# First pair of a two-layer graph network: adjacency loaded at once, evictions shared by two engines, weights loaded behind the first gather

## The chip, the cores and the metric

The kernel runs on one core of one Trainium2 chip. A time is the device time of one execution in microseconds (us). Three executions were timed; the profile is of a further one. Engines are called PE (TensorE, matmuls), DVE (VectorE), ACT (ScalarE), POOL (GpSimd) and SP (SyncE, which here only issues transfers). Each engine works through its own instructions strictly in the order in which they were built; a transfer is issued by the queue of SP, ACT or POOL.

## The reference

There are 16 graphs of 1024 nodes with 64 features each, and a symmetric 0/1 adjacency matrix in 32-bit floats (4 MB per graph). Two layers are computed; both begin with `h = max(layernorm(x), 0)` and end with `x = x + layer(h, adj)`.

```
# layer 0: a neighbourhood quantile
neigh = (adj > 0) without the diagonal;  nb = neighbours per node
skip  = ceil(nb/2) where nb > 10: every skip-th neighbour is struck out, symmetrically
s     = the features of the remaining neighbours (and the node itself), sorted per feature
agg   = 0.25*quantile(s, .25) + 0.5*quantile(s, .5) + 0.25*quantile(s, .75)
y     = relu((h + agg) @ W1 + b1) @ W2 + b2
# layer 1: three graph convolutions, each with a batch norm, then a linear map
x1 = bn1(relu(adj @ (h @ W1) + b1));  x2 = bn2(... x1 ...);  x3 = bn3(... x2 ...)
y  = relu(concat(x1, x2, x3) @ Wl + bl)
```

## The kernel before, in words

The 16 graphs are worked on in 8 pairs, `p` from 0 to 7; a graph of a pair is `x` = 0 or 1. The 1024 nodes of a graph are 8 blocks of 128 (`NT` = 8, index `t` or `u`).

`prepare(p, pools)` makes ready what the sort of a pair needs. It loads the features into `room`, computes the layer norm, stores the result in `h_d`, and then for each graph runs `prepare_one`:

1. For each of 8 blocks: load 128 rows of the adjacency (512 KB) into a tile `a`, of which there are two buffers; ACT takes the sign of it into `edge` (one byte each, L662); DVE compares it with 0 and 1 for a flag (`junk_v`, L664); PE transposes it into `ptE` (L669); ACT evicts this from PSUM into `edgeT` (L672).
2. `edgeT` is stored in `adjT_d` (1 MB, L676), and then its diagonal is struck out on DVE (L678, here called the mask of graph x), which has to wait for that store. `chunk_sums` makes partial column sums on PE (`tot`), which ACT evicts (`sums`, L648).
3. For each block: PE computes running counts (`cs`), ACT and DVE turn them into `stays` (L717, L718).
4. For each block: PE sums `q`, ACT evicts it into `edge` with a row sum `nv` (L744).
5. DVE makes sort keys (L750), PE spreads them (`keys`), and ACT compares all nodes with them, block by block (`junk`, L762). From the counts DVE computes `place` (L765), and POOL sends the rows of `edge` to `live_d` in sorted order (L770).

`find_live` (one per graph) loads these rows back (`lp`, L786, two buffers), transposes them on PE (`pt`, L796), evicts them to `liveT` on ACT (L799), and computes the counts `nvs`. `number_slots(side)` numbers the neighbours on PE (`pr`) and evicts them on ACT into `r` (L838): side 0 (`r0`, 592 columns) before the gather, side 1 (`r1`, 432 columns) beside it.

`gather_block` picks features by matmul: DVE builds selections `s` from `r` (L962), PE multiplies them with the features `hp` into `pg` (L993), ACT evicts into `g`. `sort_block` sorts `g` on DVE by a network of minima and maxima between `g` and `t` (L920) and takes the quantiles with coefficients from ACT.

The steps of the next pair's `prepare` are woven between the blocks of the current pair. The first pair has nothing to hide behind: `ahead.rest()` runs its `prepare` to the end, and only then comes `gather_block(st, 0, pools)`. A scheduler orders the instructions of each engine; the `yield`s only mark where a step ends. After the last pair's preparation, `later` runs both layers' dense part; there alone are the weights used.

The weights are loaded ahead of everything, by 53 transfers on ACT's queue in `weight`, `column`, `row` and `both`; the batch norm's factor `s` is computed from them with a square root on ACT (L530). Tiles come from pools: `g`, `t` (pool `rows`), `s`, `agg` (pool `work`) first hold something in the first gather and sort.

Of the kernel before, what the change touches and what calls it, by code (L numbers as in the profile page):

```python
# [21 lines left out]
P = 128  # L22
C = 64
HID = 128
LN_EPS = 1e-5
BN_EPS = 0.001
# [373 lines left out]
def graph_layers_kernel(ctx: ExitStack, tc: tile.TileContext, ins, out: bass.AP):  # L400
# [93 lines left out]
    def weight(name, rows, cols, twice=False):  # L494
        t = const.tile([rows * (1 + twice), cols], F32, name=f"w_{name}")
        for k in range(1 + twice):
            nc.scalar.dma_start(out=t[k * rows : (k + 1) * rows, :], in_=ins[name])
        return t

    def column(name, rows, twice=False):  # L500
        t = const.tile([rows * (1 + twice), 1], F32, name=f"c_{name}")
        for k in range(1 + twice):
            nc.scalar.dma_start(out=t[k * rows : (k + 1) * rows, :], in_=ins[name].rearrange("(p o) -> p o", o=1))
        return t

    def row(name, cols):
        t = const.tile([P, cols], F32, name=f"r_{name}")
        nc.scalar.dma_start(out=t, in_=ins[name].partition_broadcast(P))
        return t

    def both(t, src):

        nc.vector.memset(t, 0.0)
        for k in range(2):
            half = slice(k * C, (k + 1) * C)
            nc.scalar.dma_start(out=t[half, half], in_=src)


    w1 = weight("L0_gnn_W1", C, HID, True)
    w2 = weight("L0_gnn_W2", HID, C)  # L520
    b1 = column("L0_gnn_b1", HID)
    b2 = row("L0_gnn_b2", C)
    layers = []
    for i in (1, 2, 3):
        wl = const.tile([P, P], F32, name=f"wl{i}")
        both(wl, ins[f"L1_gnn_W{i}"])
        bl, g, be, m, v = (column(f"L1_gnn_{k}{i}", C, True) for k in ("b", "g", "be", "m", "v"))
        s = const.tile([P, 1], F32, name=f"bn_s{i}")
        nc.vector.tensor_scalar(s, v, BN_EPS, None, ALU.add)
        nc.scalar.activation(s, s, AF.Sqrt)  # L530
        nc.vector.reciprocal(s, s)
        nc.vector.tensor_tensor(s, s, g, ALU.mult)

        nc.vector.tensor_tensor(m, m, s, ALU.mult)
        nc.vector.tensor_tensor(be, be, m, ALU.subtract)
        layers.append((wl, bl, s, be))
    wlast = const.tile([P, 3, P], F32, name="wlast")
    for i in range(3):
        both(wlast[:, i, :], ins["L1_gnn_Wl"][i * C : (i + 1) * C, :])
    blast = row("L1_gnn_bl", C)  # L540

    biases = {}

# [36 lines left out]
        pass  # L580


    def prepare(p, pools):
# [12 lines left out]
        yield  # L596
        st.g = {}
        st.nvs = keep.tile([P, N], F32, tag="nvs", name="nvs")
# [24 lines left out]
        nc.scalar.copy(st.hp[:, 1], h)  # L623
        nc.vector.tensor_tensor(st.hp[:, 2], h, st.hp[:, 1], ALU.subtract)
        yield
        for x in range(2):
            yield from number_slots[x](1)
        return st

    def diagonal(e):  # L630

        dims = [list(d) for d in e.ap]
        return bass.AP(tensor=e.tensor, offset=e.offset, ap=[dims[0], [N + P, NT], [1, P]])
# [17 lines left out]
    def prepare_one(st, x, pools):  # L651
# [5 lines left out]
        edge = work.tile([P, NT, N], F8, tag="byte", bufs=4, name="edge")  # L657
        edgeT = work.tile([P, NT, N], F8, tag="byte", bufs=4, name="edgeT")
        for t in range(NT):
            a = work.tile([P, N], F32, tag="a", bufs=2, name="a")  # L660
            nc.sync.dma_start(out=a, in_=adj_d[b, t * P : (t + 1) * P, :])
            nc.scalar.activation(edge[:, t, :], a, AF.Sign, saturate=False)  # L662
            junk = work.tile([P, N], F8, tag="junk_v", name="junk_v")
            nc.vector.scalar_tensor_tensor(  # L664
                junk, a, 1.0, a, ALU.is_equal, ALU.not_equal, accum_out=odd[:, b, t : t + 1], saturate=False
            )
            pt = ps.tile([P, NT, P], F32, tag="big", bufs=2, name="ptE")
            for u in range(NT):
                nc.tensor.matmul(  # L669
                    out=pt[:, u, :], lhsT=edge[:, t, u * P : (u + 1) * P], rhs=ident_h, start=True, stop=True  # L670
                )
            nc.scalar.activation(edgeT[:, :, t * P : (t + 1) * P], pt, AF.Copy, saturate=False)  # L672
            if t % 2:
                yield

# [47 lines left out]
        for t in range(NT):  # L723
            q = ps.tile([P, N], F32, tag="big", bufs=2, name="q")
            for hf in range(NH):
                sl = slice(hf * HALF, (hf + 1) * HALF)
                own = slice(t * P, (t + 1) * P)
                nc.tensor.matmul(out=q[:, sl], lhsT=ident_16, rhs=stays[:, t, sl], start=True, stop=False)

                others = [sl]  # L730
                if t // 4 == hf:
                    others = [slice(sl.start, own.start), slice(own.stop, sl.stop)]
                    nc.tensor.matmul(out=q[:, own], lhsT=edgeT[:, t, own], rhs=ident_h, start=False, stop=False)
                    nc.tensor.matmul(out=q[:, own], lhsT=ident_h, rhs=ident_h, start=False, stop=False)
                for o in others:
                    if o.start < o.stop:
                        nc.tensor.matmul(out=q[:, o], lhsT=ident_h, rhs=edge[:, t, o], start=False, stop=False)
                for u in range(4 * hf, 4 * hf + 4):
                    nc.tensor.matmul(  # L739
                        out=q[:, u * P : (u + 1) * P], lhsT=stays[:, u, t * P : (t + 1) * P], rhs=ident_16,  # L740
                        start=False, stop=(u % 4 == 3),
                    )

            nc.scalar.activation(  # L744
                edge[:, t, :], q, AF.Relu, bias=bias(-2.0), accum_out=nv[:, t : t + 1], saturate=False
            )
            yield

        key = work.tile([P, NT], F32, tag="key", name="key")
# [30 lines left out]
        def find_live():  # L780
# [3 lines left out]
            for t in range(NT):  # L784
# [10 lines left out]
                for u in range(NT):  # L795
                    nc.tensor.matmul(  # L796
                        out=pt[:, u, :], lhsT=lp[:, u * P : (u + 1) * P], rhs=ident_h, start=True, stop=True
                    )
                nc.scalar.activation(liveT[:, :, t * P : (t + 1) * P], pt, AF.Copy, saturate=False)  # L799
                yield  # L800

            half = slice(x * C, (x + 1) * C)
# [22 lines left out]
            def number_slots(side):  # L825

                j0, j1 = ((0, SPLIT), (SPLIT, N))[side]
                for u in range(NT):
                    pr = ps.tile([P, N], F32, tag="big", bufs=2, name="pr")
                    for a in range(j0, j1, HALF):  # L830
                        sl, o = slice(a, min(a + HALF, j1)), slice(a - j0, min(a + HALF, j1) - j0)
                        nc.tensor.matmul(out=pr[:, o], lhsT=upto, rhs=liveT[:, u, sl], start=True, stop=(u == 0))  # L832
                        if u:
# [533 lines left out]
    with ExitStack() as stack:  # L1367
# [7 lines left out]
        with ExitStack() as inner:  # L1375
# [8 lines left out]
            gather_block(st, 0, pools)  # L1384
            for p in range(NP - 1):
                ahead = Steps(prepare(p + 1, early))
                for n in range(last + 1):
# [84 lines left out]
```

## Time and profile before

| | us |
|---|---|
| median of 3 runs | 3222.06 (3213.88 to 3228.77) |
| the profiled execution | 3236.08 |
| its span, first to last instruction | 3234.3 |
| first matmul starts | 34.1 |
| mask of graph 0 ends | 60.5 |
| `place` of graph 0 | 108.0 |
| mask of graph 1 ends | 114.9 |
| `place` of graph 1 | 159.8 |
| `nvs` of graph 1 ends | 193.6 |
| first matmul of the first gather | 204.9 |

PE is busy for 81% of the span, DVE 79%, ACT 53%, POOL 14%. These shares are means over very different stages: in the first 205 us no engine is full, in the gathers and sorts DVE and PE nearly are. A row of an engine's groups gives the busy time and the mean duration of one instruction, and after the bar the idle time before it and what ended that idle time. In the timeline, a name such as ACTq is the queue of that engine, which issues transfers.

### The profile page before, as it was taken

Reading aid. Unit: us, or ns where it says so; the run is one execution under the profiler, and the core shown is the slowest. Engines: PE = TensorE matmul, PEld = TensorE weight load, DVE = VectorE, ACT = ScalarE, POOL = GpSimd, SP = SyncE. Lnnn points to the kernel's source line nnn. Section 1 sums busy time; section 2 is a strip of 40 time slices with the busy share of each in tenths; the row PEclk is TensorE's granted clock in tenths of the full one; section 3 lists DMA queues with packets and bytes.
Section 4 is the critical chain, followed back from the end, with each engine's and each line's share of the span. In section 5 each row is a group of like instructions: output and inputs, shape, how many; then the busy total and the mean of one; then the engine's idle time right before and its main releaser. Section 6 shows DMA issues by size and latency. Waiting matters only on the chain. (4 is left out here: it accounts for less than half of the span.)

```text
span 3234.3 us, 67196 instructions
## 1 busy us (share of the span) xinstructions
PE 2614.8 (81%) x27819; PEld 1721.7 (53%) x27849; DVE 2568.1 (79%) x5895; ACT 1710.7 (53%) x3292; POOL 468.4 (14%) x545
## 2 busy tenths in 40 slices
PE   2679977997898689868695898789877689888778
PEld 2446644664566456545463566456644357555445
DVE  4149989898988989898998989898896788883332
ACT  4777647655765576556454765576553323232221
POOL 4111020111011101110211011001112120221110
PEclk9789988997998899889797999799988799898889
DMA  4132112101311031115101211131103110222211
GB/s 135 46 105 66 33 46 98 58 28 35 103 51 47 27 108 36 49 32 116 37 19 43 98 58 29 34 104 51 36 18 67 13 46 12 55 55 53 53 53 41
DMA packets 221082, 177.45 MB, mean 55 GB/s; under 512 B 189024, under 2 KB 189152, under 8 KB 216672
## 3 DMA queue, kind: packets, MB, share of 16 engines
q1 hardware_dynamic: 141824, 125.88, 12.8%
q0 software_dynamic: 17408, 37.81, 3.9%
q10 hardware_dynamic: 61536, 9.39, 1.9%
q8 instruction: 219, 3.59, 0.5%
q14 instruction: 95, 0.78, 0.1%
HBM read 124.44 MB, written 48.55 MB: 53 GB/s over the span
## 5 line engine op out<-in xcount | busy, mean ns | idle before, releaser
L993 PE MATMUL pg<-s,hp 128*64 128x400 bf16 (+11 forms) x16848 | 1379.6, 314 | 183.0 <-DVE s L962 150.6
L993 PEld LDWEIGHTS <-hp 128*64 128x64 bf16 x16848 | 906.4, 113 | 562.4 <-DVE s L962 130.9
L962 DVE TENSOR_SCALAR s<-r 128x3200 bf16<-128x3200 bf16 (+25 forms) x1312 | 620.9, 521 | 142.7 <-PE pg L993 111.1
L998 ACT COPY g<-pg 128x400 f32<-128x400 f32 (+10 forms) x384 | 169.0, 441 | 440.0 <-PE pg L993 338.3
L920 DVE TENSOR_TENSOR t<-g 128x600 f32<-128x600 f32 (+9 forms) x524 | 318.8, 629 | 11.0 <-ACT g L998 9.8
L1147 PE MATMUL pg<-adjT,xw 128*64 128x512 fp8e4 x2304 | 286.0, 400 | 35.8 <-ACT xw L1132 12.2
L770 POOL DMA_INDIRECT live_d<-edge,place x128 | 159.1, 1243 | 983.9 <-DVE place L765 835.8
L920 DVE TENSOR_TENSOR g<-t 128x96 f32<-128x96 f32 (+16 forms) x555 | 285.7, 540 | 1.8
L855 ACT ACTIVATE coef<-z,bias 128x200 f32<-128x200 f32 (+6 forms) x480 | 173.1, 401 | 149.9 <-DVE agg L933 145.4
L1147 PEld LDWEIGHTS <-xw 128*64 128x64 bf16 x2304 | 139.5, 115 | 167.9 <-issue 41.3
L1190 POOL DMA_INDIRECT agg<-agg_d,place x128 | 141.7, 1107 | 535.6 <-PE pt L1078 314.3
L920 DVE TENSOR_TENSOR t<-t 128x192 f32<-128x192 f32 (+20 forms) x447 | 209.4, 479 | 1.0
L786 POOL DMA_DIRECT2D lp<-live_d x128 | 91.4, 714 | 816.9 <-PE pt L796 779.1
L664 DVE SCALAR_TENSOR_TENSOR junk_v<-a 128x1024 fp8e4<-128x1024 f32 x128 | 156.4, 1222 | 60.9 <-DMA a<-in_adj 60.4
L858 ACT ACTIVATE coef<-coef,wcol 128x200 f32<-128x200 f32 (+7 forms) x512 | 187.4, 398 | 2.3 <-issue 1.5
L799 ACT ACTIVATE liveT<-pt 128x1024 fp8e4<-128x1024 f32 x128 | 129.8, 1024 | 103.0 <-PE pt L796 101.4
L796 PE MATMUL pt<-ident_h,lp 128*128 128x128 bf16 x1024 | 108.9, 274 | 91.9 <-DMA lp<-live_d 45.3
L832 PE MATMUL pr<-liveT,upto 128*128 128x512 fp8e4 (+2 forms) x384 | 121.5, 332 | 65.9 <-ACT r L838 56.1
L838 ACT CAST r<-pr 128x592 bf16<-128x592 f32 (+1 forms) x256 | 142.7, 585 | 51.0 <-PE pr L834 47.4
L744 ACT ACTIVATE edge<-q,bias 128x1024 fp8e4<-128x1024 f32 x128 | 142.1, 1112 | 49.6 <-PE q L739 49.2
L762 ACT ACTIVATE junk<-keys,minus 128x1024 fp8e4<-128x1024 f32 x128 | 144.3, 1128 | 41.5 <-PE keys L755 40.6
L662 ACT ACTIVATE edge<-a 128x1024 fp8e4<-128x1024 f32 x128 | 133.8, 1055 | 44.2 <-DMA a<-in_adj 43.7
(182 smaller groups left out, 3914.6 us busy)
## 6 DMA issues: line engine op xcount, KB each, us to landing
a<-in_adj SPq DMA_DIRECT2D x128, 512.0 KB
adjT_d<-edgeT SPq DMA_DIRECT2D x16, 1024.0 KB
lp<-live_d POOLq DMA_DIRECT2D x128, 128.0 KB
adjT<-adjT_d SPq DMA_DIRECT2D x16, 1024.0 KB
room<-in_x SPq DMA_DIRECT2D x16, 256.0 KB
h_d<-room SPq DMA_DIRECT2D x16, 256.0 KB
h_again<-h_d SPq DMA_DIRECT2D x16, 256.0 KB
xt<-in_x SPq DMA_DIRECT2D x16, 256.0 KB
```

The source lines that it names most:

```text
L664: nc.vector.scalar_tensor_tensor(junk, a, 1.0, a, ALU.is_equal, ALU.not_equal, accum_out=odd[:, b, t : t + 1], saturate=False)
L744: nc.scalar.activation(edge[:, t, :], q, AF.Relu, bias=bias(-2.0), accum_out=nv[:, t : t + 1], saturate=False)
L762: nc.scalar.activation(junk, keys, AF.Sign, bias=minus[:, t : t + 1], accum_out=above[:, t : t + 1], saturate=False)
L770: sent = nc.gpsimd.indirect_dma_start(out=live_d[b][:, :], out_offset=bass.IndirectOffsetOnAxis(ap=place[:, b, t : t + 1], axis=0), in_=ed ...
L838: nc.scalar.copy(st.r[side][:, x, u, :], pr[:, : j1 - j0])
L855: nc.scalar.activation(coef[:, i, :], z[:, at], AF.Abs, bias=bias(rank - (slots + 1) // 2 + tau), scale=sign)
L858: nc.scalar.activation(coef[:, i, :], coef[:, i, :], AF.Relu, bias=wcol[:, q : q + 1], scale=-w)
L920: nc.vector.tensor_tensor(view(bufs, o, n1, n2), view(bufs, a, n1, n2), view(bufs, b, n1, n2), ALU.max if op else ALU.min)
L962: nc.vector.tensor_scalar(s[:, k, :, us, w0:], r[:, :, us, at + w0 : at + W], float(LIVE + 1 + k0 + k), None, ALU.is_equal)
L993: summed = nc.tensor.matmul(out=pg[x * C : (x + 1) * C, ks, w0:], lhsT=st.hp[:, part, x, u, :], rhs=s[:, ks, x, u, w0:], start=(whole and ...
L998: nc.scalar.copy(g[:, k0 : k0 + n, :], pg)
L1147: nc.tensor.matmul(out=pg[cs, :], lhsT=part[:, u, cs], rhs=adjT[x][:, u, sl], start=(u == 0 and k == 0), stop=(u == NT - 1 and k == len(xw ...
```

## The change

For the first pair alone, 16 tiles named `home` are taken, before anything else, from the buffers of `g` (twice 2 blocks), `t` (3), `s` (twice 3), `agg` (1) and `a` (twice 1), one for each block of its two graphs, and all 16 loads are issued on SP's queue one after the other; `prepare_one` then takes `a` from there. A helper `evict` sends the odd blocks of `edgeT`, `liveT` and `r` to DVE where there are homes, and `edge` (L744) likewise; the even blocks and all other pairs stay on ACT. The 53 loads of the weights move from ACT's queue to SP's, and their place in the program from the beginning to behind the first `gather_block`, with the three batch norm factors. The instructions of later pairs are otherwise as before, except that `r` is evicted on ACT by an activation with Copy in place of a copy.

```diff
     def weight(name, rows, cols, twice=False):
...
-            nc.scalar.dma_start(out=t[k * rows : (k + 1) * rows, :], in_=ins[name])
+            nc.sync.dma_start(out=t[k * rows : (k + 1) * rows, :], in_=ins[name])
...
-    w1 = weight("L0_gnn_W1", C, HID, True)
...
-    blast = row("L1_gnn_bl", C)
...
+    def evict(st, t, o, i):
+
+        if st.homes and t % 2:
+            nc.vector.tensor_scalar(o, i, 1.0, None, ALU.mult, saturate=o.dtype != F8)
+        else:
+            nc.scalar.activation(o, i, AF.Copy, saturate=o.dtype != F8)
...
-            a = work.tile([P, N], F32, tag="a", bufs=2, name="a")
-            nc.sync.dma_start(out=a, in_=adj_d[b, t * P : (t + 1) * P, :])
+            if st.homes:
+                a = st.homes[x * NT + t]
+            else:
+                a = work.tile([P, N], F32, tag="a", bufs=2, name="a")
+                nc.sync.dma_start(out=a, in_=adj_d[b, t * P : (t + 1) * P, :])
...
-            nc.scalar.activation(edgeT[:, :, t * P : (t + 1) * P], pt, AF.Copy, saturate=False)
+            evict(st, t, edgeT[:, :, t * P : (t + 1) * P], pt)
...
-            nc.scalar.activation(
-                edge[:, t, :], q, AF.Relu, bias=bias(-2.0), accum_out=nv[:, t : t + 1], saturate=False
-            )
+            if st.homes and t % 2:
+                nc.vector.tensor_scalar(
+                    edge[:, t, :], q, 3.0, 0.0, ALU.is_equal, ALU.add, accum_out=nv[:, t : t + 1], saturate=False
+                )
+            else:
+                nc.scalar.activation(
+                    edge[:, t, :], q, AF.Relu, bias=bias(-2.0), accum_out=nv[:, t : t + 1], saturate=False
+                )
...
-                nc.scalar.activation(liveT[:, :, t * P : (t + 1) * P], pt, AF.Copy, saturate=False)
+                evict(st, t, liveT[:, :, t * P : (t + 1) * P], pt)
...
-                    nc.scalar.copy(st.r[side][:, x, u, :], pr[:, : j1 - j0])
+                    evict(st, u, st.r[side][:, x, u, :], pr[:, : j1 - j0])
...
-            ahead = Steps(prepare(0, early))
+            work, _, rows = pools
+            homes = []
+            for pool, tag, bufs, free in (
+                (rows, "g", 2, 2), (rows, "g", 2, 2), (rows, "t", 1, 3), (work, "s", 2, 3), (work, "s", 2, 3),
+                (work, "agg", 1, 1), (early[0], "a", 2, 1), (early[0], "a", 2, 1),
+            ):
+                home = pool.tile([P, free, N], F32, tag=tag, bufs=bufs, name="home")
+                homes += [home[:, k] for k in range(free)]
+            for k, home in enumerate(homes):
+                nc.sync.dma_start(out=home, in_=adj_d[k // NT, k % NT * P : (k % NT + 1) * P, :])
+
+            ahead = Steps(prepare(0, early, homes))
             ahead.rest()
             st = ahead.result
             gather_block(st, 0, pools)
+
+            w1 = weight("L0_gnn_W1", C, HID, True)
...
+                nc.vector.tensor_scalar(s, v, BN_EPS, None, ALU.add)
+                nc.scalar.activation(s, s, AF.Sqrt)
...
+            blast = row("L1_gnn_bl", C)
```

More of the change, by code (lines that the diff above doesn't have):

```diff
@@ L502, in column @@
         for k in range(1 + twice):
-            nc.scalar.dma_start(out=t[k * rows : (k + 1) * rows, :], in_=ins[name].rearrange("(p o) -> p o", o=1))
+            nc.sync.dma_start(out=t[k * rows : (k + 1) * rows, :], in_=ins[name].rearrange("(p o) -> p o", o=1))
         return t
@@ L507, in row @@
         t = const.tile([P, cols], F32, name=f"r_{name}")
-        nc.scalar.dma_start(out=t, in_=ins[name].partition_broadcast(P))
+        nc.sync.dma_start(out=t, in_=ins[name].partition_broadcast(P))
         return t
@@ L515, in both @@
             half = slice(k * C, (k + 1) * C)
-            nc.scalar.dma_start(out=t[half, half], in_=src)
-    w1 = weight("L0_gnn_W1", C, HID, True)
[L520 to L539, printed above, removed]
-    blast = row("L1_gnn_bl", C)
+            nc.sync.dma_start(out=t[half, half], in_=src)
     biases = {}
@@ L580, in graph_layers_kernel, with prepare @@
         pass
-    def prepare(p, pools):
+    def prepare(p, pools, homes=()):
         work, keep, ps = pools
@@ L597, in prepare @@
         st.g = {}
+        st.homes = homes
         st.nvs = keep.tile([P, N], F32, tag="nvs", name="nvs")
@@ L1384, in graph_layers_kernel @@
             gather_block(st, 0, pools)
+            w1 = weight("L0_gnn_W1", C, HID, True)
+            w2 = weight("L0_gnn_W2", HID, C)
+            b1 = column("L0_gnn_b1", HID)
+            b2 = row("L0_gnn_b2", C)
+            layers = []
+            for i in (1, 2, 3):
+                wl = const.tile([P, P], F32, name=f"wl{i}")
+                both(wl, ins[f"L1_gnn_W{i}"])
+                bl, g, be, m, v = (column(f"L1_gnn_{k}{i}", C, True) for k in ("b", "g", "be", "m", "v"))
+                s = const.tile([P, 1], F32, name=f"bn_s{i}")
+                nc.vector.tensor_scalar(s, v, BN_EPS, None, ALU.add)
+                nc.scalar.activation(s, s, AF.Sqrt)
+                nc.vector.reciprocal(s, s)
+                nc.vector.tensor_tensor(s, s, g, ALU.mult)
+                nc.vector.tensor_tensor(m, m, s, ALU.mult)
+                nc.vector.tensor_tensor(be, be, m, ALU.subtract)
+                layers.append((wl, bl, s, be))
+            wlast = const.tile([P, 3, P], F32, name="wlast")
+            for i in range(3):
+                both(wlast[:, i, :], ins["L1_gnn_Wl"][i * C : (i + 1) * C, :])
+            blast = row("L1_gnn_bl", C)
             for p in range(NP - 1):
```

## The prediction

> **What bounds the kernel now.** The change touches the first pair alone, so I read the page only for the whole (PE 81%, DVE 79%, neither full) and then the first 250 us by stage. The table by stage gives, for each stretch, its length and the busy time of PE, PE's weight loads, DVE, ACT and POOL, then granted clock, DMA share and GB/s:
>
> ```profile
> 0.00:25.00 25.00, 0.00 (x0) 0.00 (x0) 11.42 (x116) 1.69 (x3) 20.25 (x55) 1.00 0.32 74
> 25.00:50.00 25.00, 6.12 (x48) 4.62 (x48) 9.66 (x18) 14.31 (x16) 19.71 (x83) 1.00 0.52 153
> 75.00:100.00 25.00, 17.41 (x174) 12.91 (x172) 1.47 (x5) 20.05 (x31) 0.00 (x0) 0.91 0.00 1
> 150.00:175.00 25.00, 16.17 (x91) 8.08 (x91) 2.87 (x4) 20.09 (x30) 11.16 (x13) 0.59 0.40 112
> 225.00:250.00 25.00, 23.10 (x310) 15.95 (x308) 22.07 (x30) 18.10 (x30) 0.00 (x0) 1.00 0.31 105
> ```
>
> In the first 25 us ACT and PE do nothing; from 75 to 175 ACT works 20 of 25 us and DVE 1.5 to 5; from 225 on DVE and PE carry. Three limits follow each other: something holds ACT until 32 us, then the adjacency trickles in, then ACT's evictions pace. The waits of the first 60 us and ACT's timeline name the first two:
>
> ```profile
> PE ptE L669 <- ACT edge L662: 44.6, 7, 34.1
> ACT L530 <- DMA c_L_gnn_b<-in_L_gnn_b: 15.2, 1, 15.2
> DVE junk_v L664 <- DMA a<-in_adj: 12.3, 10, 2.1
> ...
> 31.44 0.59 ACTq L508 DMA_DIRECT2D r_L_gnn_bl<-in_L_gnn_bl  x1
> 32.08 1.06 ACT L561 ACTIVATE room<-room 128x1024 f32<-128x1024 f32 x1 [1.73 <-DMA wlast<-in_L_gnn_Wl]
> 33.05 1.99 ACT L662 ACTIVATE edge<-a 128x1024 fp8e4<-128x1024 f32 x2
> ```
>
> ACT issues 53 weight loads, some 0.6 us each, before its first sign at 33.05. Then `a`, with two buffers, makes everyone wait for loads: DVE's compares start about 2.3 us apart (43.72, 45.96, 48.39, 50.68), where they last 1.23. The third limit, between `keys` and `place` of graph 0:
>
> ```profile
> 98.28 1.11 ACT L762 ACTIVATE junk<-keys,minus 128x1024 fp8e4<-128x1024 f32 x1
> 99.27 0.20 ACT L762 ACTIVATION_READ_ACCUMULATOR junk<-keys,minus 128x1 f32 x1
> 99.48 1.02 ACT L672 ACTIVATE edgeT<-ptE 128x1024 fp8e4<-128x1024 f32 x1
> 100.40 1.11 ACT L762 ACTIVATE junk<-keys,minus 128x1024 fp8e4<-128x1024 f32 x1
> ```
>
> ACT is gapless: 1.20 for a compare, 0.92 for an eviction that lies between.
>
> **What the skill says.** (1) "DMA: Bandwidth & Descriptors", section "Issuing engines are not separate DMA queues": several issuing engines only save sequencer time. The trace agrees: the weights move little, yet cost ACT's sequencer 31 us. (2) The same page, "Bandwidth": 341 GB/s for 1 MB, 425 for 16 MB. Here 512 KB loads, two in flight, reach 274 to 332 GB/s in single us with the engines full (36 to 42 us), and 228 on average when one comes every 2.3 us. (3) "VectorE: DVE Perf Modes", "Why PSUM operands drop a tier": 32-bit PSUM operands run at one element per cycle. No run of before has a one-tensor DVE operation on a large PSUM tile; the nearest rows are two tensors, one in PSUM, 512 elements, 0.689 us (L1135), and one tensor in SBUF, 1024 elements, 0.69 (L611). An eviction of 1024 lies between 0.69 and 1.22; I take 1.22. (4) "ScalarE: Activation LUTs", "What ACT_TABLE_LOAD costs": 1.28 us and a drain; the trace has one, 1.283. The changed program has two.
>
> **Part A, the start: -22.0 us to the mask of graph 0.** Built, the changed program has on SP the 16 home loads first, then `room`, `mk`, the store of `edgeT`; on DVE all 16 compares, 4 evictions, then layer norm and mask. ACT's first sign waits for nothing but a home. Removed: 31 us of issuing and the buffers' wait; what is late next is DVE or the loads.
> DVE: first home as late as the first `room` pair (issued 0.77, used 4.81), taken 4.6; 16 compares each 1.27 (60.55 to 61.82) 20.3; 4 evictions at 1.22 (1067 ns for 1024 elements plus the 0.155 by which 0.689 exceeds 512 elements) 4.9; ident and other constants, memsets of weights and some 70 biases (28 took 0.79) 4.1; together 33.9. Layer norm's three (1.22, 0.2, 1.23) to 36.6.
> Loads: homes 8.39 MB, `room` 0.52 and store 1.05 in one queue, 9.96 MB; at 276 to 332 GB/s 30 to 36 us, behind 2.8 of latency: 33 to 39. I take a mask start of 37.3, so an end of 38.5 against 60.5. Bounds: at 228 GB/s 46.5, end 47.7, gain 12.8; at 360 DVE decides, end 37.8, gain 22.7.
>
> **Part B, mask to `place` of graph 0 (now 47.5): -2.9.** Four signs of graph 1 leave ACT's queue between the `stays`. Graph 1 shows that stretch without them: mask end to key takes 26.8 (114.9 to 141.7), graph 0 29.25: -2.4. Four evictions of `edgeT` leave ACT: 4 x 0.92 = -3.7; DVE, idle 17.87 before `place`, hides them. Moving half of `edge` (L744) gains nothing: PE makes a `q` every 1.44, and ACT's 1.3 is beneath it.
> Added: the three square roots stand in ACT's queue after the 2nd and 8th `stays` and the 2nd even `edge`; behind each wait all `stays` or `edge` of ACT, then PE for want of PSUM, and DVE's matching `add` blocks DVE too. Each needs `c_v`, on SP behind `h_d` (issued once layer norm ends, 3.1 after the mask; 1.0 for two), behind graph 1's `mk` (waits for `act`, 4.2), then 5 issues at 0.35 to 0.6 and 2 us of landing: 8.3 to 9.5 after the mask, ACT being there at 7.2. So +2.0 with the root. The next comes 12 issues later, at 12.5 to 16.7 against ACT's 15.5, the third at 16.7 to 23.9 against 22: together +1.2. Sum +3.2; bounds 0.6 (three roots of 0.2) and 10 (issues of 0.85). The second table load falls into ACT's idle time around the mask: nothing; uncovered 1.3.
>
> **Part C, to the mask of graph 1: +0.3.** The last `edgeT` is DVE's, at 1.22 instead of 1.02. SP has issued all weights by then (28 after the mask against 44), so the store is not held up.
>
> **Part D, to `place` of graph 1: -2.2.** Three evictions of `liveT` fewer before the last compare (2.76) and, by graph 0's pattern, one more beside it (0.7), but the next pair's `room` square and `ln_var` now stand inside this stretch (1.05 and 0.3 less overlap, 1.2).
>
> **Part E, `place` to gather: +1.0.** The 33.8 to `nvs` stay: POOL's 8 sends and reloads of `lp` rule. Behind it DVE has now, ahead of its first `s`: `half` 1.4, `z` 3.65, four `r0` at 0.77, two features' differences 1.22 each, two `r1` at 0.6: 11.8, plus 0.97 for `s`, 12.8 against 11.2: +1.5. Against this PE has six more `r1` blocks behind it by then. DVE's other six `r1` (3.6) fall into a stretch where PE rules; bounds -1 and +4.
>
> All behind the first gather keeps its order on PE, DVE, POOL and SP, so the shift goes through. 224 later evictions by Copy (some 15 ns each) lie on ACT, 53% busy: nothing.
>
> **Sum:** -22.0 - 2.9 + 0.3 - 2.2 + 1.0 = -25.8, against the profiled 3236.1 3210.3. That execution lies 14 above the median of the runs; from the median 3222.1 this makes **3196.3**.
>
> **Rivals.**
> R1, loads pace: if the queue keeps the old 228 GB/s, part A is -12.8, the sum -16.6: 3205. For it: no stretch shows more than two loads in flight. Against: full-share us above 274.
> R2, DVE takes it back: part E at +4 and waits of B at 10 give -16.0: 3206. For it: DVE has 22 of 25 busy after 225. Against: 15.8 of 25 from 200 to 225.
> R3, slower: the batch norm's loads block ACT. The third `c_v` comes 6.5 + 29 d after the mask, d being one issue on SP; ACT wants it at 22. The excess eats the gain without waits (29.0) from d = 1.53 us; at 2.1, as SP's slowest `mk` issue late in the kernel (2.13), it is 45.4, net +16.4: 3238. Against: 0.33 for SP's early `mk`, 0.6 for these loads on ACT.
> R4, homes not idle: if a `g` or `s` buffer were still held, the first gather would wait. Homes are read by 35 us, the gather comes at 180: nothing.
>
> **Chances.** 0.5% is 16.1 us, about what a measurement of this kernel can tell from no change. Forecast with its neighbours (gain 20 to 33) 0.68; R1, R2 and mixtures (gain 8 to 20) 0.27, of which 0.10 above 16.1; smaller or none 0.02; R3 0.03. Faster 0.78, same 0.19, slower 0.03. The range, 3181 to 3212, runs from -33 (loads at 360, no waits, -1 in E, and 0.25% of spread of the runs) to the weak end of R1 and R2 with the same spread.
>
> **What would show it.** First matmul before 12 us (was 34.1); home landings 1.6 to 1.9 apart; mask 0 ending at 36 to 42; DVE without 2 us waits on loads. ACT `junk` in runs of three; a wait ACT `stays` or L1401 from `c_v` of 1 to 3 us; `place` at 83 and 133, first `pg` near 179. Wrong: a mask after 47, SP issues of `c_v` above 1 us, or a first `pg` after 190.

## The result, and the profile of the kernel after

The median of the kernel after is 3195.98 us (3194.95 to 3196.71), that of the kernel before, run beside it, 3222.82 (3213.88 to 3228.77): a ratio of 0.9919, 95% interval 0.9895 to 0.9942. A second set of runs gave 0.9946 (0.9926 to 0.9965). The gain is small, 0.8% and 0.5%, but both intervals lie below 1. The forecast of 3196.3 is met to a third of a microsecond. Its steps are not. The first gather starts 12.6 us earlier than before, not 25.8; the rest of the gain of the first set lies in the 3000 us behind it, and what made it is only in part known.

The table by stage of the kernel after, columns as above, for the same stretches:

```profile
0.00:25.00 25.00, 7.62 (x64) 6.90 (x65) 21.10 (x86) 18.97 (x20) 15.27 (x43) 1.00 0.95 354
25.00:50.00 25.00, 10.38 (x71) 6.05 (x71) 17.32 (x72) 10.03 (x12) 22.23 (x74) 1.00 0.29 76
75.00:100.00 25.00, 9.86 (x89) 6.84 (x89) 7.20 (x13) 12.82 (x19) 8.34 (x9) 0.57 0.23 85
150.00:175.00 25.00, 15.16 (x111) 8.50 (x109) 8.71 (x10) 9.40 (x12) 4.37 (x8) 0.70 0.16 48
225.00:250.00 25.00, 23.69 (x259) 14.47 (x257) 23.97 (x38) 16.74 (x19) 0.00 (x0) 0.93 0.24 85
```

In the first 25 us the DMA engines are 0.95 busy and move 354 GB/s (0.32 and 74 before); DVE works 21 of 25, ACT 19. That is the intended start. In the two stretches shown between 75 and 175 no engine is busy for more than 15.2 of 25 us, and the granted clock is 0.57 and 0.70. The waits of the first 180 us (waiting line, releaser, us in total, times, longest) show what replaced the old ones:

```profile
PE ptE L657 <- DVE ident_h L417: 9.8, 1, 9.8
DVE bn_s L1400 <- DMA c_L_gnn_v<-in_L_gnn_v: 5.6, 3, 4.2
ACT stays L705 <- DMA h_d<-room: 5.4, 1, 5.4
```

PE's first wait ends at 9.8 us, where it was 34.1. The other two rows stand between the mask and `place` of graph 0; ACT's timeline has them in place (start, length, what was idle before and its releaser):

```profile
44.16 2.12 ACT L705 ACTIVATE stays<-cs,back 128x1024 f16<-128x1024 f32 x2 [5.38 <-DMA h_d<-room]
62.90 0.20 ACT L1401 ACTIVATE bn_s<-bn_s 128x1 f32<-128x1 f32 x1 [2.73 <-DVE bn_s L1400]
68.65 1.11 ACT L737 ACTIVATE edge<-q,bias 128x1024 fp8e4<-128x1024 f32 x1 [4.46 <-PE q L727]
```

The third row is what the second causes: while ACT and DVE stand at the third root, PE runs out of PSUM, and the next `edge` waits for a late `q`.

Step by step, in us, from the two profiled executions:

| stretch | before | after | change | forecast |
|---|---|---|---|---|
| A: start to end of mask 0 | 60.5 | 35.8 | -24.7 | -22.0 |
| B: to `place` of graph 0 | 47.5 | 51.3 | +3.8 | -2.9 |
| C: to end of mask 1 | 6.9 | 8.2 | +1.3 | +0.3 |
| D: to `place` of graph 1 | 44.9 | 43.9 | -1.0 | -2.2 |
| E: to `nvs`, then to the first `pg` of pair 0 | 33.8 + 11.2 | 34.3 + 18.8 | +8.1 | +1.0 |
| sum, at the first `pg` | 204.9 | 192.3 | -12.6 | -25.8 |

### The profile page after: what moved, and what is told of

It is laid out like the page before. It is cut to its first block, busy times and chain, and to the rows that moved or that the text cites. A ratio compares the mean times of both kernels' runs of the same rounds, so it can differ in the third digit from the quotient of the medians.

```text
span 3194.9 us, 67204 instructions
## 1 busy us (share of the span) xinstructions
PE 2606.3 (82%) x27849; PEld 1723.4 (54%) x27849; DVE 2604.8 (82%) x5943; ACT 1680.9 (53%) x3245; POOL 457.5 (14%) x545
## 5 line engine op out<-in xcount | busy, mean ns | idle before, releaser
L986 PE MATMUL pg<-s,hp 128*64 128x400 bf16 (+11 forms) x16848 | 1365.1, 314 | 183.9 <-DVE s L955 164.5
L779 POOL DMA_DIRECT2D lp<-live_d x128 | 83.7, 655 | 807.8 <-PE pt L789 774.8
L652 DVE SCALAR_TENSOR_TENSOR junk_v<-a 128x1024 fp8e4<-128x1024 f32 x112 | 136.7, 1220 | 42.1 <-DMA a<-in_adj 41.5
L613 ACT ACTIVATE liveT<-pt 128x1024 fp8e4<-128x1024 f32 x120 | 121.6, 1024 | 93.1 <-PE pt L789 90.3
L613 ACT ACTIVATE r<-pr 128x592 bf16<-128x592 f32 (+1 forms) x240 | 135.6, 593 | 55.6 <-PE pr L827 49.4
L737 ACT ACTIVATE edge<-q,bias 128x1024 fp8e4<-128x1024 f32 x120 | 133.2, 1112 | 57.6 <-PE q L727 57.4
L705 ACT ACTIVATE stays<-cs,back 128x1024 f16<-128x1024 f32 x128 | 136.7, 1113 | 41.9 <-DVE look L686 23.4
```

The lines of the kernel that those rows point to most:

```text
L613: nc.scalar.activation(o, i, AF.Copy, saturate=o.dtype != F8)
L986: summed = nc.tensor.matmul(out=pg[x * C : (x + 1) * C, ks, w0:], lhsT=st.hp[:, part, x, u, :], rhs=s[:, ks, x, u, w0:], start=(whole and ...
```

## The experiments

Times of kernels that ran at different times are not comparable: the kernel before had medians of 3222.8, 3234.5, 3197.2, 3196.2 and 3223.4 in the five sets. So each kernel is judged by its ratio to the runs of before beside it, and by where its landmarks stand in its profile, which repeat far better: up to `place` of graph 1, two profiles of the kernel after agree within 0.4 us and two of before within 1.5. The kernels, in the order of their sets, with times in us:

| kernel | mask 0 starts | `place` 0 | `place` 1 | `nvs` 1 to first `pg` | first `pg` | ratio to before (95%) |
|---|---|---|---|---|---|---|
| before | 59.3 | 108.0 | 159.8 | 11.2 | 204.9 | 1 |
| after | 34.6 | 87.1 | 139.2 | 18.8 | 192.3 | 0.9919 (0.9895 to 0.9942) |
| weights_only | 34.8 | 85.7 | 137.5 | 11.3 | 182.3 | 0.9936 (0.9918 to 0.9954) |
| homes_only | 58.8 | 105.0 | 156.6 | 12.4 | 203.5 | 0.9999 (0.9986 to 1.0013) |
| no_dve | 29.2 | 83.4 | 135.7 | 12.7 | 182.5 | 0.9925 (0.9895 to 0.9954) |
| before_again | 60.3 | 109.5 | 160.7 | 10.3 | 204.2 | 1.0005 (0.9995 to 1.0015) |
| own_room | 30.8 | 84.7 | 137.1 | 19.2 | 190.7 | 0.9920 (0.9895 to 0.9946) |
| roots_first | 36.8 | 86.0 | 138.0 | 18.3 | 190.5 | 0.9959 (0.9947 to 0.9972) |
| late8 | 34.3 | 86.8 | 150.7 | 17.9 | 201.2 | 0.9978 (0.9966 to 0.9990) |
| best | 30.7 | 89.1 | 141.2 | 12.1 | 187.0 | 0.9936 (0.9907 to 0.9964) |
| best_room_first | 36.5 | 83.0 | 136.0 | 12.1 | 182.1 | 0.9928 (0.9910 to 0.9945) |
| after_again | 34.2 | 87.2 | 139.2 | 18.3 | 191.8 | 0.9946 (0.9926 to 0.9965) |
| late8_again | 34.3 | 85.5 | 149.5 | 17.9 | 200.4 | 0.9983 (0.9971 to 0.9994) |
| store_between | 29.4 | 78.0 | 129.7 | 11.2 | 174.3 | 0.9890 (0.9872 to 0.9909) |

**Which part carries the gain: weights_only, homes_only, no_dve.**

weights_only, the kernel before with

```diff
-            nc.scalar.dma_start(out=t[k * rows : (k + 1) * rows, :], in_=ins[name])
+            nc.sync.dma_start(out=t[k * rows : (k + 1) * rows, :], in_=ins[name])
...
             gather_block(st, 0, pools)
+            w1 = weight("L0_gnn_W1", C, HID, True)
...
```

> The kernel before, with the weight loads alone moved behind the first gather and onto SP; adjacency still through the two buffers `a`, all evictions on ACT. Theory 1 (ACT's 31 us of issuing was the whole of part A's stall, the two buffers only its second limit): the first sign comes at 4 to 6 us instead of 33.05, and as the old kernel needed 27.5 us from there to the end of mask 0, the mask ends at 32 to 36, as early as with everything (35.8): median 12 to 25 us under before. Rival (the homes are needed, since the loads trickle at 2.3 us each and the 53 weight issues on SP delay them): the mask ends after 45 and the median is less than 10 us under before.

The first sign starts at 6.72, the mask at 34.8, as early as with the whole change, and the first `pg` comes 10 us before that of the kernel after. Theory 1 holds, but for a first sign a little later than 4 to 6. By ratio the gain is 0.0064 x 3234.5 = 20.7 us, what the landmarks say (22.6).

homes_only, the kernel after with

```diff
-            nc.sync.dma_start(out=t[k * rows : (k + 1) * rows, :], in_=ins[name])
+            nc.scalar.dma_start(out=t[k * rows : (k + 1) * rows, :], in_=ins[name])
...
-        if st.homes and t % 2:
+        if False:
             nc.vector.tensor_scalar(o, i, 1.0, None, ALU.mult, saturate=o.dtype != F8)
```

the same `False` where DVE would take half of `edge`, and the weights' loads put back at the start of the program.

> The kernel after, with the weight loads back at the start on ACT's queue and every eviction on ACT: only the 16 homes are left of the change. Theory 1: ACT's first sign stays at 33; eight signs and eight evictions at 1.0 and 0.92 us follow without a wait for a load, so mask 0 ends at 48 to 52 (60.5 before) and the median is 6 to 12 us under before. Rival (the homes are the larger part): mask 0 at 40 or earlier, median 15 or more under before.

Neither came. ACT's issuing, now beside 8 MB of homes, lasted until 36.8 (32.0 before). From ACT's first sign to the mask's end it then took 23.2 us instead of 27.5, so the homes do shorten that stretch, but the later first sign took nearly all of it back: the mask came 0.5 earlier than in the kernel before. Here the loads slowed the issuing that everybody waited for.

no_dve, the kernel after with

```diff
-        if st.homes and t % 2:
+        if False:
             nc.vector.tensor_scalar(o, i, 1.0, None, ALU.mult, saturate=o.dtype != F8)
...
-            if st.homes and t % 2:
+            if False:
                 nc.vector.tensor_scalar(
                     edge[:, t, :], q, 3.0, 0.0, ALU.is_equal, ALU.add, accum_out=nv[:, t : t + 1], saturate=False
```

> The kernel after, with every eviction and all of `edge` of the first pair on ACT again. Theory 1: part A was paced by DVE, so without its four evictions mask 0 ends 0 to 5 us earlier than 35.8, unless ACT's 16 signs and 8 evictions (23.7 us from 4) pace instead: 33 to 37. From mask to `place` of graph 0 the evictions of graph 1 stand between ACT's compares again, +3 to +5. In part E `r0` and `r1` leave DVE: nvs to the first pg back from 16 to about 11 us. Sum against the kernel after: -4 to +4. Rival (evictions on DVE carry the gain): 8 us or more over the kernel after.

The mask ends at 30.4, earlier than the 33 to 37 expected: DVE's four evictions, 4.9 us, had held it back. Eight evictions instead of four between ACT's compares cost 2.6 (15.9 against 13.3 from the first compare to `place`), and the first `pg` follows `nvs` in 12.7 instead of 18.8. So up to the gather moving evictions to DVE was worth less than nothing. The ratio, 0.9925, cannot be told from that of the kernel after.

**Is a landmark's shift what the end sees: before_again, late8, after_again, late8_again.**

before_again is the kernel before, unchanged.

> The kernel before, unchanged, for a second profile. Between the two first profiles the lead of the changed kernel grew from 14.4 us at graphs 2 to 5 to 27 at pair 7 and 39.4 at the end, in a stretch whose instructions have the same order on PE, DVE, POOL and SP. Theory 1 (that growth is spread between executions of one program, by where the windows of half clock fall): this profile's `place` of the later graphs differs from the first profile's by 5 to 15 us while the first two graphs agree within 1. Rival (the growth belongs to the change): they agree within 3 us to the end, and so does the span (3234).

The rival came nearer: `place` stays within 1.5 of the first profile for 13 of 16 graphs and 3.3 for the last three, the span within 4.2 (3238.5 and 3234.3).

late8, the kernel after with

```diff
-        for t in range(NT):
+        for t in list(range(NT)) * (2 if st.homes and x else 1):
             junk = work.tile([P, N], F8, tag="junk", name="junk")
```

> The kernel after, with the eight compares behind `keys` of graph 1 run twice (the same result twice), which only delays the first pair by 8 times 1.2 us = 9.6 at most. Theory 1 (later pairs have a fixed length at full clock, some 283 us each, and what differs is what the windows of half clock take in each, 23.9 to 27.3; where they fall depends on when the pair starts): `place` of graph 1 comes 7 to 10 later than in the kernel after, yet later pairs and the end shift by another amount, 3 or more away from it, and lengths less the clock's loss stay within 2 us pair by pair. Rival (a shift goes through unchanged): the distance at `place` of graph 1 is kept within 2 us to the end, median 8 to 10 over the kernel after.

`place` of graph 1 is 11.5 later, yet the profiled span is 0.9 shorter than that of the kernel after, which seemed to speak for theory 1. But the two ran in different sets, so both were run once more together.

> The kernel after, unchanged, on the chip of the other two. Theory 1 (the place of the half-clock windows repeats from run to run of one program): `place` of graphs 0 and 1 within 1 us of 87.1 and 139.2, and the stretch from graph 1's to graph 3's `place` again 5 to 9 longer than in the kernel before, with 8 to 12 more lost to the clock. Rival (that loss was an accident of one execution): that stretch is 242, as before.

> late8 once more beside the kernel after on one chip, since chips differ by more than its effect. Theory 1 (a delay at the start is partly taken back by where the windows fall): its median is within 5 of the kernel after, though `place` of graph 1 is 10 to 12 later. Rival (a shift goes through): 9 to 12 over the kernel after.

Run together, `place` of graph 1 is 10.3 later, the first `pg` 8.6 and the profiled span 8.4; the medians differ by 15.8 us, the ratios by 0.0037, 11.8 us. Nothing is taken back: the shift goes through, and theory 1 of late8 falls. after_again bears out theory 1 of its own expectation: both `place` agree within 0.1 with the first profile, and the stretch from graph 1's to graph 3's is 248.9 (249.4 in the first profile, 242.1 before), with 25.9 lost to the clock (26.1, and 15.6 before). Loss means the length of each stretch times one minus its granted clock, added up over the trace's own stretches of full and half clock, since the two digits of the table are too coarse. The mean clock can be read from the table by stage; here from `place` of graph 1 to that of graph 3, and from there to the end, in the kernels before, after and after_again:

```profile
159.80:401.90 242.10, 215.26 (x2384) 138.52 (x2387) 186.34 (x278) 165.82 (x285) 28.32 (x32) 0.94 0.22 68
401.90:3234.30 2832.40, 2326.31 (x24777) 1531.00 (x24799) 2334.24 (x5426) 1447.48 (x2882) 387.94 (x360) 0.90 0.18 52
```
```profile
139.20:388.50 249.30, 222.25 (x2394) 141.32 (x2395) 199.80 (x297) 153.40 (x262) 25.87 (x32) 0.90 0.20 66
388.50:3194.90 2806.40, 2308.63 (x24803) 1527.88 (x24799) 2332.63 (x5425) 1447.89 (x2881) 378.21 (x360) 0.90 0.18 52
```
```profile
388.10:3171.10 2783.00, 2281.07 (x24805) 1516.45 (x24801) 2334.24 (x5426) 1445.54 (x2882) 386.52 (x360) 0.91 0.19 53
```

The third busy time in each row is DVE's, 2334.24 in two of the three long stretches and 2332.63 in the other: the work is the same. PE's, the first, is not: 2326, 2309, 2281. From graph 3 on the loss is 289.5 in before, 271.3 in after and 240.8 in after_again; the stretch less the loss is 2542.9, 2535.1 and 2542.2. So the clock goes the way of the time, but the sum does not come out exactly: between the two profiles of one program the loss differs by 30.5 and the time by 23.4, and of the 26.0 us that the first profile of after gained on before here, 18.2 are loss and 7.8 are not explained. The two profiles of one program also come from different sets, and between these the median of the kernel before itself moved by 26.6 us.

**The two waits of stretch B, and the version to keep: own_room, roots_first, best, best_room_first, store_between.**

own_room, the kernel after with

```diff
-        room = work.tile([P, 4, 2, NT, C], F32, tag="stays", name="room")
+        where, tag = (keep, "r0") if homes else (work, "stays")
+        room = where.tile([P, 4, 2, NT, C], F32, tag=tag, name="room")
```

> The kernel after, with `room` of the first pair in the idle buffer of `r0` instead of the one it shares with `stays`. Theory 1 (the first `stays` waited 5.4 us because its buffer was still being stored as h_d): that wait is gone, ACT's first `stays` follows mask 0's end by 5 us or less instead of 8.4, and the stretch from mask 0 to `place` of graph 0, 52.5 us from the mask's start, is 3 to 6 shorter; the layer norm also leaves the place ahead of the mask on DVE, so the mask comes 2 to 3 earlier; `place` of graph 0 at 78 to 82 (87.1). Rival (the wait only covers those for `c_v` behind it, which then take its place): `place` at 84 to 87.

The wait is gone: the first `stays` comes 5.2 behind the mask's end, not 8.4. But `place` comes at 84.7, as the rival had it. The new buffer lies where the setup's `bounds` lines lie, whose last load POOL issues at 52.8, and SP's load of `room` waited for it; so `room` was loaded from 55.5 on, and DVE stood 4.9 us ahead of the layer norm with `edge` and `key` behind it.

roots_first, the kernel after with

```diff
+            for i in (1, 2, 3):
+                v = column(f"L1_gnn_v{i}", C, True)
+                s = const.tile([P, 1], F32, name=f"bn_s{i}")
+                nc.vector.tensor_scalar(s, v, BN_EPS, None, ALU.add)
+                nc.scalar.activation(s, s, AF.Sqrt)
+                nc.vector.reciprocal(s, s)
+                roots.append(s)
             work, _, rows = pools
             homes = []
```

> The kernel after, with the three `c_v` columns (six loads) and their square roots ahead of the homes, so that no root stands between `stays` and `edge`; the other weights unchanged. Theory 1 (the third `c_v` held DVE for 4.2 and ACT for 2.7, the first two 1 to 2 together): mask 0 starts 1 to 3 later than 34.6, for the six issues ahead of the homes, and the stretch to `place` is 3 to 5 shorter than 52.5; `place` of graph 0 at 84 to 87. Rival (PE, not the wait, paced the `edge` stretch): it stays at 51 or more, and `place` at 88 to 90.

As theory 1 says: the mask 2.3 later, the stretch from its end to `place` 48.0 instead of 51.3, and within it the eight `edge` 11.6 instead of 15.1. The third root cost 3.5 us. By ratio, 0.9959, no gain on the kernel after can be seen.

best, the kernel after with the edits of the last two and

```diff
-            evict(st, t, edgeT[:, :, t * P : (t + 1) * P], pt)
+            evict(st, t * x, edgeT[:, :, t * P : (t + 1) * P], pt)
...
-                    evict(st, u, st.r[side][:, x, u, :], pr[:, : j1 - j0])
+                    nc.scalar.copy(st.r[side][:, x, u, :], pr[:, : j1 - j0])
...
-                junk, a, 1.0, a, ALU.is_equal, ALU.not_equal, accum_out=odd[:, b, t : t + 1], saturate=False
+                junk, a, st.one if x and st.homes else 1.0, a, ALU.is_equal, ALU.not_equal,
+                accum_out=odd[:, b, t : t + 1], saturate=False,
```

where `st.one` is a column of ones made from graph 0's `look`.

> What the runs so far point to: the kernel after, with `room` in r0's buffer, the three roots first, graph 0's `edgeT` on ACT (DVE keeps those of graph 1 and `liveT`), graph 1's eight compares held back until graph 0's `look` is there, `r` on ACT by Copy of the old form. Theory 1 (DVE's 16 compares, then the two waits, set the first 87 us): mask 0 starts at 21 to 25, `place` of graph 0 at 68 to 74 and of graph 1 at 119 to 126, against 87.1 and 139.2; if half of that shift reaches the end, the median is 8 to 18 under the kernel after. Rival (ACT's 16 signs and 8 evictions, 24 us, pace the start just as well, and the held-back compares slow `edge`): `place` of graph 0 at 80 or later.

The rival's number, and half of its mechanism: ACT's signs and evictions ended only at 26.4, the store of `edgeT` was issued behind them at 26.43, and the mask waited for it. Then `one`, like `room`, lay in the setup's memory and waited until 54.2 for it.

best_room_first, the kernel after with `r` on ACT as in best, `one` in `const`, and

```diff
+            def load():
+                for k, home in enumerate(homes):
+                    nc.sync.dma_start(out=home, in_=adj_d[k // NT, k % NT * P : (k % NT + 1) * P, :])
+                    if k == NT - 1:
+                        for i in (1, 2, 3):
+                            v = column(f"L1_gnn_v{i}", C, True)
...
-        nc.sync.dma_start(out=adjT_d[b][:, :, :], in_=edgeT)
+        if st.homes and x == 0:
+            nc.scalar.dma_start(out=adjT_d[b][:, :, :].bitcast(F32), in_=edgeT[:, :, :].bitcast(F32))
+        else:
+            nc.sync.dma_start(out=adjT_d[b][:, :, :], in_=edgeT)
```

where the three roots follow their columns as in roots_first, and `prepare` calls `load` behind the layer norm's code.

> The run named best kept its mask waiting for the store of `edgeT` (30.7, no earlier than own_room), and its held-back compares and `room` waited until 54 for the setup's last bounds load, whose memory their new buffers lay in. This kernel is the one after, with: `room` loaded ahead of the homes in its old buffer, so that h_d is stored before `stays`; the roots' columns between graph 0's homes and graph 1's; graph 0's `edgeT` evicted on ACT and its store issued on ACT's queue instead of behind graph 1's homes; graph 1's compares held back by a column made from graph 0's `look` in memory of its own; `r` on ACT. Theory 1 (store, DVE's 16 compares and the two waits set the first 87 us): mask 0 at 22 to 27, `place` of graph 0 at 68 to 75 (87.1), of graph 1 at 120 to 127 (139.2), and the median under the kernel after by half or more of that, 6 to 16. Rival (ACT paces, and the held-back compares slow `stays`): `place` of graph 0 at 80 or later, median within 5 of the kernel after.

Both waits are gone (stretch B 45.3, first `stays` 5.2 behind the mask), but the mask is no earlier: ACT's last eviction of graph 0 ended at 26.6, the store was issued at 26.65, and another queue did not bring it past the homes. `r` on ACT brings the first `pg` 12.1 behind `nvs`.

store_between, that kernel with `evict(st, t, ...)` for `edgeT` as in the kernel after and

```diff
         nc.sync.dma_start(out=adjT_d[b][:, :, :], in_=edgeT)
+        if st.homes and x == 0:
+            st.load(1)
...
-            nc.scalar.activation(edge[:, t, :], a, AF.Sign, saturate=False)
+            if x and st.homes:
+                nc.scalar.activation(edge[:, t, :], a, AF.Sign, bias=nil, saturate=False)
+            else:
+                nc.scalar.activation(edge[:, t, :], a, AF.Sign, saturate=False)
```

where `nil` is a column of zeros made from graph 0's `look`.

> In all kernels with homes the mask of graph 0 started between 29 and 37, whatever was ahead of it on DVE and ACT, and in best and best_room_first DVE's wait ahead of it ended with the store of `edgeT`, which shares the engines with graph 1's homes. This kernel is best_room_first with graph 0's `edgeT` evicted by ACT and DVE in turn as in the kernel after, its store on SP behind graph 0's homes (one home of graph 1 slips ahead of it), graph 1's homes behind that, and graph 1's signs, like its compares, held back until graph 0's `look` is there. Theory 1 (the store, not DVE, sets the mask): the store is issued at 20 to 22, the mask starts at 24 to 27 (34.6), ACT's first `stays` follows by 31, and `place` comes at 69 to 76 for graph 0 (87.1) and 121 to 129 for graph 1 (139.2); the median is 6 to 16 under the kernel after. Rival (eight signs between `stays` and `edge`, and compares on DVE beside them, cost as much as the mask gains): `place` of graph 0 at 80 or later though the mask is early.

The mask starts at 29.4, later than the 24 to 27 hoped for, since the store was issued at 23.9; `place` of graph 0 at 78.0 lies between theory and rival. DVE's mask in best, best_room_first and store_between, each from that kernel's DVE timeline:

```profile
30.68 1.22 DVE L671 TENSOR_TENSOR edgeT<-edgeT,other_h 128x1024 fp8e4<-128x1024 fp8e4 x1 [11.33 <-DMA adjT_d<-edgeT]
```
```profile
36.48 1.23 DVE L672 TENSOR_TENSOR edgeT<-edgeT,other_h 128x1024 fp8e4<-128x1024 fp8e4 x1 [9.57 <-DMA adjT_d<-edgeT]
```
```profile
29.38 1.23 DVE L676 TENSOR_TENSOR edgeT<-edgeT,other_h 128x1024 fp8e4<-128x1024 fp8e4 x1 [2.53 <-DMA adjT_d<-edgeT]
```

The mask writes `edgeT` in place, so it waits for the store that reads it: 9.8 us from issue to mask where the homes compete for the engines, 5.5 with most of them behind it, 4.3 in best, where the last home had been issued 8 us before. This kernel's first `pg` comes at 174.3, 30.6 before that of before, and its ratio, 0.9890, is the lowest of all. It lies under the intervals of after_again and weights_only; against the first runs of the kernel after (0.9919) the intervals overlap, so a lead of 9 us over that is likely, not shown.

## Why the prediction was right in its sum and wrong in its steps

**Part A** was the right mechanism, a little too small: -24.7 for -22.0. DVE paced, as chosen, at 1.27 for a compare and 1.22 for an eviction of 128x1024. The Trainium skill ("VectorE: DVE Perf Modes", "Why PSUM operands drop a tier") has 32-bit operands in PSUM at one element per cycle, and the trace agrees: evictions of 1024, 592 and 432 elements took 1.22, 0.78 and 0.61 us, about 1.03 ns for each further element, where an operation on one 32-bit tensor of 1024 in SBUF took 0.69. The loads did not hold it up: 354 GB/s over 25 us, above the 276 to 332 assumed and a little above the 341 that "DMA: Bandwidth & Descriptors", "Bandwidth", gives for 1 MB. R1 falls. But the part's credit went to the wrong edit: weights_only has the mask as early. The homes remove a limit that the evictions moved to DVE put back: without these, in no_dve, the mask starts at 29.2.

**Part B** failed by 6.7, in three terms. The waits, priced at +3.2, are 2.9 for one not foreseen (from the mask's end to the first `stays` 8.4 instead of 5.5) and 3.9 for the third root (the eight `edge` take 15.1 instead of 11.2). `room` and `stays` share one buffer; I took the layer norm behind 16 compares as harmless, and did not ask who needs `room` back. `h_d` is issued at 38.86, and ACT's first `stays` waits for its landing. The third `c_v` was forecast by its issue time, 6.5 + 29 d with d = 0.6 read off ACT's queue; d was 0.62 on SP, but SP was through with `h_d` and `mk` only at 42.2, 6.4 behind the mask's end where I had 4.5, and issued that column at 59.33:

```profile
38.86 1.01 SPq L572 DMA_DIRECT2D h_d<-room  x2
39.97 2.18 SPq L640 DMA_DIRECT2D mk<-in_nodemask  x1
59.33 1.23 SPq L503 DMA_DIRECT2D c_L_gnn_v<-in_L_gnn_v  x2
```

So R3's mechanism is real, in its small form: 3.5 us by roots_first. The evictions leaving ACT were to bring -3.7 and bring -2.6 (15.9 to 13.3 from the first compare to `place`): DVE's third eviction stands right ahead of `place`. The signs' departure, -2.4, brings 0.5 in the eight `stays` (11.6 to 11.1); in homes_only it brings 2.1 (9.5). Why it does not in the kernel after was not tried.

**Parts C and D** are 1.0 and 1.2 worse than worked out. C is 8.2 to 8.6 in every kernel where DVE evicts graph 1's last `edgeT`, and 6.9 in every one where ACT does. D was not taken apart.

**Part E** failed by 7.1, beyond its bound of +4, and is R2: DVE takes it back. I summed DVE's instructions from `nvs` to the first `s` as if each could start; they could not. The sum itself was right, 11.8 us of work, but DVE stood 3.5 us between them. And the first `pg` came 3.5 behind the start of `s`, not 1.0: PE's blocks of `r1`, which I had booked as a credit, stood ahead of it and waited for ACT's evictions. DVE's timeline in after and in store_between:

```profile
176.74 1.21 DVE L592 SCALAR_TENSOR_TENSOR z<-nvs,half 128x1024 f32<-128x1024 f32 x1
178.93 0.78 DVE L611 TENSOR_SCALAR r<-pr 128x592 bf16<-128x592 f32 x1 [0.98 <-PE pr L827]
179.62 1.22 DVE L592 SCALAR_TENSOR_TENSOR z<-nvs,half 128x1024 f32<-128x1024 f32 x1
181.81 0.78 DVE L611 TENSOR_SCALAR r<-pr 128x592 bf16<-128x592 f32 x1 [0.98 <-PE pr L827]
...
188.73 0.98 DVE L955 TENSOR_SCALAR s<-r 128x3200 bf16<-128x3200 bf16 x1
```
```profile
164.62 3.50 DVE L597 SCALAR_TENSOR_TENSOR z<-nvs,half 128x1024 f32<-128x1024 f32 x3
171.22 1.23 DVE L605 TENSOR_TENSOR h_again<-h_again,hp 128x1024 f32<-128x1024 f32 x1 [3.10 <-ACT hp L604]
172.36 1.89 DVE L968 TENSOR_SCALAR s<-r 128x3200 bf16<-128x3200 bf16 x2
```

With `r` in turn on ACT and DVE, each `z` waits behind an eviction that waits for PE, whose next block waits for the other engine's eviction: DVE, ACT and PE go in step, two blocks in 2.88 us (178.93, 181.81), and `s` starts 15.3 behind `half` (173.45). With `r` on ACT alone, the three `z` run on, and `s` starts 9.2 behind it. All six profiles with `r` in turn have 17.9 to 19.2 from `nvs` to `pg`; all eight with it on ACT, whatever else they evict on DVE, 10.3 to 12.7. This was the term to price by its waits.

The two groups differ in a second thing, the clock granted in this stretch. From `nvs` to the first `pg` in after and in store_between, columns as in the tables by stage:

```profile
173.40:192.30 18.90, 14.46 (x49) 5.42 (x50) 13.99 (x17) 14.55 (x31) 0.59 (x3) 0.52 0.17 55
163.10:174.30 11.20, 7.63 (x38) 3.37 (x38) 7.97 (x9) 10.28 (x20) 2.45 (x3) 0.84 0.15 47
```

It is 0.52 to 0.59 in the six profiles and 0.71 to 1.00 in the eight, and the stretch less its loss is 9.0 to 10.7 us in all fourteen. Going in step costs something at the same clock too: while store_between was at half clock, two evictions of `r` on ACT came 0.99 apart,

```profile
165.69 0.65 ACT L844 CAST r<-pr 128x592 bf16<-128x592 f32 x1 [0.34 <-PE pr L840]
166.68 0.65 ACT L844 CAST r<-pr 128x592 bf16<-128x592 f32 x1 [0.34 <-PE pr L840]
```

so 2.0 for two blocks against 2.88 in step. Over the eight blocks of `r0` this makes, by estimate, 3.6 of the 7.6 us between the two kernels. Whether going in step also kept the clock low, or the low clock added the rest on its own, no run separates.

**Why the sum still came out.** By luck. The ratio's gain of the kernel after was 26.1 us (19 to 34) in the first set and 17.3 (11 to 24) in the second, against 12.2 and 12.7 by the landmark at the first `pg` (taking 204.5 for before). For ten of the twelve changed kernels with a ratio, gain by ratio and shift of the first `pg` agree within 6 us; the first set of after and own_room exceed it by 12 to 14. So that the shift goes through held in most, and late8_again shows it; but my 25.8 met 26.8 because 13 us of error in the steps met an excess of that size, which no step had foreseen and of which the second set has 5. My own mark for "wrong", a first `pg` after 190, was reached: 192.3.

Where the excess comes from stays open. In the first profiles of before and after, the loss behind the first `pg` is 291.0 and 275.9, so 15 of the 27 us gained there go with the clock. But the four timed runs of after in that set, with mean clocks of 0.901, 0.901, 0.895 and 0.898, lie within 1.8 us of each other, so the mean clock alone does not settle the time; and no run here moved the clock at will.

Four slips of the forecast and the text ahead of it changed little. The loads of the weights are 48, not 53. ACT works 14 us, not 20, in the stretch from 100 to 125. Of the six single us read for the rate of the loads, two had 193 and 204 GB/s. And the lower end of the range adds up to -31.7 before the spread, not -33.

## What to carry to other kernels

Before pricing a move of work between engines, list for each moved instruction what it waits for in its new queue and what stands behind it there: evictions of one PSUM ring given in turn to two engines tie both and the producer to one another's waits. Here a lower granted clock went with it, and only part of the loss could be given to the one of them. Before letting a step come later, ask which tile shares its buffer and which store reads it. And test a compound change by its parts, in one set with the kernel before: here one of three parts, moving the weights, carried the gain, and its companions paid for themselves only once the store, the roots and `r` were put right as well.

## What the runs showed of the hardware

Sixteen 512 KB loads, issued one after the other on one queue, brought the DMA engines to 354 GB/s at a share of 0.95 over the first 25 us, where two buffers let one load through every 2.3 us, 228 GB/s; but issuing them took SP 14.2 us, and a 1 MB store issued on another engine's queue while eight of them were under way still took 9.8 us to release its tile. Column loads of 0.2 KB cost SP 0.62 us each, nearly as much as a 512 KB home (0.57 to 0.89). And one program's profiles, 3171.1 and 3194.9, agreed within 0.4 us at 388 and differed by 23.8 at the end; the loss to the granted clock from there on, 240.8 and 271.3 us, differs by more than that, and the kernel before moved by as much between the same two sets.
